# Local attention rebuilt: q and k made by features, their lengths spread from DRAM, tokens weighed instead of values

## The chip, the core and the metric

The kernel runs on one NeuronCore of a Trainium2 chip. The core has a matrix engine (TensorE, "PE" in the profile, its weight loads "PEld"), VectorE ("DVE"), ScalarE ("ACT"), GpSimd ("POOL") and a queue engine (SyncE, "SP") that here issues all DMAs. The engines run side by side; each takes its own instructions strictly in the order of the program and waits on semaphores for the others. Matrix products land in PSUM (eight banks of 2 KB per partition), everything else is in SBUF (128 partitions). The metric is device time in microseconds (us) of one execution.

## The reference

`x` is [8, 512, 128]: 8 batches, 512 tokens, 128 features, all float32. Two blocks follow each other:

- `x = x + LN(attention(LN(x)))`: 16 heads with a Taylor-expanded kernel (1 + s + s²/2, causal). The change doesn't alter its arithmetic.
- `x = x + LN(six layers(LN(x)))`. Each layer is a local attention and a feed-forward, on tokens shifted by one in half of the features:

```
for i in range(6):
    x = attn_layer(shift_tokens(x)) + x
    x = ffn_layer(shift_tokens(x)) + x
attn_layer: q, k, v = split(x @ Wqkv)            # 16 heads of 64
            q = l2norm(q) * qs; k = l2norm(k) * ks
            q = q*cos*scale + rotate_half(q)*sin*scale     # k with 1/scale
            window of 32 tokens: each token sees its window and the one before
            attn = softmax(8 * q k^T, masked);  out = attn @ v;  return out @ Wo
ffn_layer:  (LN(x) @ W1 + b1) -> a * gelu(gate) @ W2 + b2   # inner width 341
```

## The kernel before, in words

**Two stages.** The first (to about 479 us) is the Taylor attention, `slot` and what it calls. The second walks 192 units: 6 layers x 8 batches x 4 blocks of 128 tokens. The state is kept by features in SBUF (`state[b]`, 128 features x 513), so that a shift of tokens is an offset of one column.

**The order.** For TensorE the order is written out by hand: the loop over `t` at the end of the kernel. In turn `t`, `at(t, lag, step)` runs `step` for unit `t - lag`, so several units are in flight, one step each. For the other engines a list scheduler places the instructions; a tile pool gives each tile a buffer by its tag, and an instruction that needs a buffer waits for the last reader of the tile that was there. PSUM has the tags `mm` (two buffers of two banks), `s` (one buffer of two banks: scores, weighed values) and `tr` (two of one bank).

**One unit before**, in turns 0 to 3:

- `proj` (L439): q and k by tokens, four products of 128x128 by 512 columns (L451). VectorE multiplies them by the two tables of the rotation (`turned` L459, `straight` L467), ScalarE squares them (L475; it waits for `straight`), GpSimd adds the two (L482).
- `values` and `spread`: v by tokens (L509), copied by ScalarE (L514) and dealt out by eight DMAs into windows.
- `sum_squares` (VectorE, L485), `unit_length`: a root by logarithm and exponential (L96, L98), a clamp on GpSimd (L495), and q and k times it on GpSimd (L498).
- `by_features`: 16 transposes on TensorE (L70) and four ScalarE copies (L548) bring q and k to features.
- `masked` (L558): ScalarE writes the mask into PSUM; `scores` (L572): 64 small products per unit added onto it; VectorE takes the maxima (L580), 16 exponentials on ScalarE (L584) with the maximum as bias, VectorE the sums (L590).
- `by_keys`: 8 transposes of the weights on TensorE and two copies (L602). `weigh_values`: 64 small products with v (L613), VectorE divides by the sums (L621).
- `out_by_features`: 8 more transposes and two copies (L635). `out_project`: 8 products (L642), VectorE adds to the state (L647).
- After a batch's fourth block: `feed_norm`, `feed_first`, `feed_middle`, `feed_last`, in four turns that follow each other (lags 3 to 6), with Gelu tables loaded and unloaded on ScalarE.

Padding instructions (`addr_align`, lines 668, 671, 780, 782) stand between some matrix products.

Of the kernel before, what the change touches and what calls it, by code (L numbers as in the profile page):

```python
# [8 lines left out]
F32 = mybir.dt.float32  # L9
# [14 lines left out]
FILL = 16  # L24
IN_STEP = 98
# [3 lines left out]
def sandwich_kernel(ctx: ExitStack, tc: tile.TileContext, ins: dict, out: bass.AP):  # L29
# [5 lines left out]
    DEPTH = ins["L0_ffn_Wqkv"].shape[0]  # L35
# [16 lines left out]
    x1 = [dram.tile([P, NB, DM], F32, tag=f"x1_{b}", name=f"x1_{b}") for b in range(B)]  # L52
    roots = [dram.tile([2, 2, 2, N], F32, tag=f"roots_{i}", name=f"roots_{i}") for i in range(2)]
    state = [const.tile([P, N + 1], F32, tag=f"state_{b}", name=f"state_{b}") for b in range(B)]
    for b in range(B):
        nc.vector.memset(state[b][HD:P, 0:1], 0.0)
# [3 lines left out]
    vec = const.tile([P, NV + 1], F32, tag="vec", name="vec")  # L60
    g_c, b_c, b2_c = (vec[:, i * DEPTH : (i + 1) * DEPTH] for i in range(3))
    b1_c = vec[:, 3 * DEPTH : NV].rearrange("p (c l) -> p c l", l=DEPTH)
    gw = vec[:, NV : NV + 1]

# [8 lines left out]
    tables, exps, divisions, copies, pcopies, maxima = [], [], [], [], [], []  # L73
# [7 lines left out]
    def gelu_only():  # L81
        ld = nc.scalar.preload_act_table_set("gelu_and_others")
        issue_behind(ld, pcopies[-1])
        issue_behind(ld, exps[-1])
        tables.append(ld)
# [51 lines left out]
    fq = ctx.enter_context(tc.tile_pool(name="fq", bufs=2))  # L137

    HF = HD // 2
# [13 lines left out]
    tw = wl.tile([P, 3, 2, 512], F32, tag="wqkv", name="tw")  # L153
# [4 lines left out]
    nc.sync.dma_start(tw[:, 2], a_w[:, 2])  # L158
# [3 lines left out]
    woT = tw[:, 2].rearrange("p s (c d) -> p (s c) d", d=DM)  # L162
# [10 lines left out]
    for a in range(2):  # L173
        nc.vector.memset(of[HD * a : HD * (a + 1), a::2], 1.0)
    eps4 = const.tile([P, 1], F32, tag="eps4", name="eps4")
# [54 lines left out]
    def project_qk(G):  # L230
        b, g = divmod(G, NQ)
        k = f2.tile([P, 2, N], F32, tag="pe", name=f"tk_{G}")[:, 0]
        q = fq.tile([P, N], F32, tag="tq", name=f"tq_{G}") if g % 2 == 0 else gr[G - 1]["q"]
        gr[G]["q"], gr[G]["k"] = q, k
        for s, dst in ((0, q), (1, k))[g % 2 :]:
            cols = slice(g * P, (g + 1) * P) if s else slice(g // 2 * P, (g // 2 + 1) * P)
            ps = psum.tile([P, N], F32, tag="tr", name="qk")
            nc.tensor.matmul(ps, wqk[:, s, cols], bt[b]["xlT"], start=True, stop=True)
            nc.scalar.copy(dst, ps)
# [160 lines left out]
    rot = const.tile([P, 4, NB, HD], F32, tag="rot", name="rot")  # L400
    nc.sync.dma_start(rot, ins["rotary"].rearrange("k (n p) d -> p k n d", p=P))
    qks = const.tile([P, 2, DEPTH, HD], F32, tag="qks", name="qks")
    for s, nm in enumerate(("q_scale", "k_scale")):
        nc.sync.dma_start(
            qks[:, s].rearrange("p l d -> p (l d)"),
            ins[f"L0_ffn_{nm}"].rearrange("l d -> (l d)").partition_broadcast(P),
        )

    def load_layer(l):
        wqkv = wl.tile([P, 3, 2, 512], F32, tag="wqkv", name=f"wqkv_{l}")  # L410
        nc.sync.dma_start(
            wqkv, ins["L0_ffn_Wqkv"][l].rearrange("p (t s c) -> p t s c", t=3, s=2)
        )
        wo = wl.tile([P, NP, DM], F32, tag="wo", name=f"wo_{l}")
        nc.sync.dma_start(wo, ins["L0_ffn_Wo"][l].rearrange("(c p) d -> p c d", p=P))
# [7 lines left out]
        tab = wl.tile([P, 4, NB, HD], F32, tag="tab", name=f"tab_{l}")  # L423
        for s in range(2):
            sc = qks[:, s, l, :]
            nc.gpsimd.tensor_tensor(
                tab[:, 2 * s], rot[:, 2 * s], sc.unsqueeze(1).to_broadcast([P, NB, HD]), ALU.mult
            )
            for a, o in ((0, HF), (HF, 0)):
                nc.gpsimd.tensor_tensor(  # L430
                    tab[:, 2 * s + 1, :, a : a + HF],
                    rot[:, 2 * s + 1, :, a : a + HF],
                    sc[:, o : o + HF].unsqueeze(1).to_broadcast([P, NB, HF]),
                    ALU.mult,
                )

        return dict(wqkv=wqkv, wo=wo, w1=w1, w2=w2, tab=tab)

    def proj(u, s):  # L439

        L, b, j = u["L"], u["b"], u["j"]
        wqkv, tab = L["wqkv"], L["tab"]
        lhs = state[b][:, j * P : (j + 1) * P]
        if s == 0:
            u["ss"] = f2.tile([P, 2, H], F32, tag="ss", name="ss")
            u["qk"] = f2.tile([P, 2, H, 2, HF], F32, tag="qk", name="qk")
        ss, qk = u["ss"], u["qk"]

        ps = psum.tile([P, 2, H, HF], F32, tag="mm", name="mm")
        for a in range(2):  # L450
            nc.tensor.matmul(  # L451
                ps[:, a].rearrange("p h d -> p (h d)"), lhs, wqkv[:, s, a, :], start=True, stop=True
            )
        sq = f2.tile([P, H, 2, HF], F32, tag="sq", name="sq")
        t1 = f2.tile([P, 2, H, HF], F32, tag="t1", name="t1")
        t2 = f2.tile([P, 2, H, HF], F32, tag="t2", name="t2")

        def turned():
            nc.vector.tensor_tensor(  # L459
                t2, ps[:, ::-1],  # L460
                tab[:, 2 * s + 1, j, :].rearrange("p (a d) -> p a d", a=2).unsqueeze(2)
                .to_broadcast([P, 2, H, HF]),
                ALU.mult,
            )

        def straight():
            nc.vector.tensor_tensor(  # L467
                t1, ps,
                tab[:, 2 * s, j, :].rearrange("p (a d) -> p a d", a=2).unsqueeze(2)
                .to_broadcast([P, 2, H, HF]),  # L470
                ALU.mult,
            )

        def squared(a):
            nc.scalar.activation(sq[:, :, a, :], ps[:, a], AF.Square)  # L475

        turned()
        straight()
        squared(0)
        squared(1)  # L480
        u["sq", s] = sq
        nc.gpsimd.tensor_tensor(qk[:, s].rearrange("p h a d -> p a h d"), t1, t2, ALU.add)  # L482

    def sum_squares(u, s):
        su = nc.vector.tensor_reduce(  # L485
            u["ss"][:, s], u["sq", s].rearrange("p h a d -> p h (a d)"), AX.X, ALU.add
        )
        if divisions:
            issue_behind(su, divisions[-1])

    def unit_length(u):

        ss, qk = u["ss"], u["qk"]
        inverse_root(ss, ss)
        nc.gpsimd.tensor_scalar(ss, ss, 1e12, None, ALU.min)  # L495
        for i in range(2):
            t = qk[:, i].rearrange("p h a d -> p h (a d)")
            nc.gpsimd.tensor_tensor(  # L498
                t, t, ss[:, i, :].unsqueeze(2).to_broadcast([P, H, HD]), ALU.mult
            )  # L500

    def values(u):
        L, b, j = u["L"], u["b"], u["j"]
        lhs = state[b][:, j * P : (j + 1) * P]

        v0 = f3.tile([P, 2, 512], F32, tag="v0", name="v0")
        ps = psum.tile([P, 2, 512], F32, tag="mm", name="mm")
        for p in range(2):
            nc.tensor.matmul(ps[:, p, :], lhs, L["wqkv"][:, 2, p, :], start=True, stop=True)  # L509
        u["v0"], u["v0ps"] = v0, ps  # L510

    def spread(u):
        j, v0 = u["j"], u["v0"]
        cp = nc.scalar.copy(v0, u.pop("v0ps"))  # L514
        if copies:
            issue_behind(cp, copies[-1])

        v2 = f2.tile([P, 4, 512], F32, tag="v2", name="v2")
        for p in range(2):
            if j == 0:  # L520
                nc.gpsimd.memset(v2[HD * p : HD * p + W, 0, :], 0.0)
            else:
                nc.sync.dma_start(v2[HD * p : HD * p + W, 0, :], u["B"]["v0"][P - W : P, p, :])
            nc.sync.dma_start(v2[HD * p + W : HD * (p + 1), 0, :], v0[0:W, p, :])
            for w in range(1, 4):
                nc.sync.dma_start(
                    v2[HD * p : HD * (p + 1), w, :], v0[W * (w - 1) : W * (w + 1), p, :]
                )
        u["B"]["v0"] = v0
        u["v2"] = v2  # L530

    def by_features(u, c, which=(0, 1)):

        j, qk, B_ = u["j"], u["qk"], u["B"]
        if c == 0:
            u["qT"] = f1.tile([P, NP, P], F32, tag="qT", name="qT")
            if j == 0:
                B_["kT"] = f2.tile([P, NP, W + P], F32, tag="kT", name="kT")
                nc.gpsimd.memset(B_["kT"][:, :, :W], 0.0)
            u["kT"] = B_["kT"]  # L540
        for s in which if isinstance(which, tuple) else (which,):
            ps = psum.tile([P, 4, P], F32, tag="tr", name="tr")
            for i in range(4):
                h0 = 2 * (c + i)
# [384 lines left out]
```

## Time and profile before

| | |
|---|---|
| time, 3 runs | 3640.79 us median (3638.26 to 3641.88) |
| profiled execution | span 3641.2 us; no other time of it is given |
| first stage | 0 to 479 us (first L451 at 479.0) |
| 192 units | 515 us per layer of 32 units, 16.09 us per unit |
| last L451 to the end | 3564.7 to 3641.2: 77 us |
| PE / DVE / ACT / POOL busy | 98 / 77 / 76 / 51 % |
| DMA | 250.73 MB, mean 69 GB/s; the kernel's own queue 240.93 MB in 25.2% of 16 engines' span |
| tr, 32 per unit (L70) | qk 440.9, pe 217.5, on 209.7 us |

A matrix product in float32 appears as two instructions (two passes), a transpose as one. "Busy" of a group is the time with at least one of its instructions running; the mean is that of one instruction, and they overlap, so a group's busy time and the spacing of starts say what it costs, not the mean. After the bar stands the idle time of the engine before the group, with what ended it. In the timeline a line gives start, duration, engine, line and count; in brackets what it had waited for.

### The profile page before, as it was taken

What the parts mean: (1) busy time and instruction counts of PE and PEld (TensorE: products, weight loads), DVE (VectorE), ACT (ScalarE), POOL (GpSimd) and SP (SyncE); (2) the same over time, 40 slices, a digit from 0 to 9 for tenths busy, and PEclk for the clock granted to TensorE, in tenths of its full rate; (3) what the DMA queues carried; (4) which work ended last, traced back from release to release, by engine and by line L of the source; (5) the groups of instructions that cost most, each with busy time, mean ns of one, the idle gap of its engine ahead of it and who ended that gap; (6) DMA issues with size and microseconds to landing.
All of it is one profiled execution on the core that took longest, in us unless ns stands there. A gap on an engine that the chain in (4) does not pass through costs nothing.

```text
span 3641.2 us, 153034 instructions
## 1 busy us (share of the span) xinstructions
PE 3575.2 (98%) x65184; PEld 2404.3 (66%) x65184; DVE 2796.4 (77%) x3915; ACT 2765.6 (76%) x6864; POOL 1843.6 (51%) x1311
## 2 busy tenths in 40 slices
PE   8999989999999999999999999999999999999997
PEld 4555556666766666676766766667676676766765
DVE  4555567887878788787887878878787887878885
ACT  4555557787888888888787888888878787887875
POOL 0000045555655556555565655556555565556652
PEclk9999999999999999999999999999999999999998
DMA  3121132222232222232222322223222222222221
GB/s 109 46 53 47 42 89 68 65 65 69 79 77 72 65 64 71 77 81 68 61 69 68 87 72 69 65 65 86 71 71 69 60 70 64 66 68 73 74 74 47
DMA packets 158598, 250.73 MB, mean 69 GB/s; under 512 B 33774, under 2 KB 54508, under 8 KB 157164
## 3 DMA queue, kind: packets, MB, share of 16 engines
q1 hardware_dynamic: 157932, 240.93, 25.2%
q8 instruction: 530, 8.68, 1.0%
q14 instruction: 136, 1.11, 0.1%
HBM read 41.31 MB, written 4.46 MB: 13 GB/s over the span
## 4 chain that ended last, share of the span: by engine, by line
PE 87%; ACT 9%; DVE 2%; issue 1%; DMA 1%; POOL 0%; SPq 0%; POOLq 0%; DVEq 0%; ACTq 0%
PE tr L70 19%; PE mm L451 14%; PE py L642 10%; PE mm L509 9%; PE po L613 8%; PE sp L572 6%; ACT pe L584 4%; PE mm L667 4%; PE mm L669 4%; PE y L299 3%; PE py L702 3%; PE sc L269 2%; PE po L348 2%; ACT L76 1%; PE vv L247 1%; ACT oT L635 1%
## 5 line engine op out<-in xcount | busy, mean ns | idle before, releaser
L482 POOL TENSOR_TENSOR qk<-t,t 128x1024 f32<-128x1024 f32 x384 | 910.9, 2372 | 619.1 <-DVE t L467 424.7
L498 POOL TENSOR_TENSOR qk<-qk,ss 128x1024 f32<-128x1024 f32 x384 | 722.4, 1902 | 16.0
L451 PE MATMUL mm<-wqkv,state 128*128 128x512 f32 x1536 | 700.3, 596 | 0.6 <-issue 0.6
L584 ACT ACTIVATE pe<-sp,mx 128x64 f32<-128x64 f32 x3072 | 652.0, 381 | 2.4 <-DVE mx L580 2.3
L459 DVE TENSOR_TENSOR t<-mm,tab 128x1024 f32<-128x1024 f32 x384 | 468.3, 1219 | 220.3 <-PE mm L451 214.9
L475 ACT ACTIVATE sq<-mm 128x512 f32<-128x512 f32 x768 | 420.6, 605 | 127.4 <-DVE t L467 120.9
L467 DVE TENSOR_TENSOR t<-mm,tab 128x1024 f32<-128x1024 f32 x384 | 468.1, 1219 | 5.9
L451 PEld LDWEIGHTS mm<-wqkv,state 128*128 128x128 f32 x1536 | 273.1, 190 | 289.8 <-issue 242.4
L485 DVE TENSOR_REDUCE ss<-sq 128x16 f32<-128x1024 f32 x384 | 448.4, 1209 | 0.1
L70 PE MATMUL tr<-ident,qk 128*128 128x128 f32 x3072 | 440.9, 276 | 1.8 <-ACT qT L548 0.8
L70 PEld LDWEIGHTS tr<-ident,qk 128*128 128x128 f32 x3072 | 351.3, 141 | 120.7 <-issue 56.3
L642 PE MATMUL py<-oT,wo 128*128 128x128 f32 x3072 | 379.3, 277 | 0.3 <-ACT oT L635 0.3
L642 PEld LDWEIGHTS py<-oT,wo 128*128 128x128 f32 x3072 | 368.1, 196 | 0.5 <-ACT oT L635 0.5
L509 PE MATMUL mm<-wqkv,state 128*128 128x512 f32 x768 | 362.9, 595 | 2.6 <-DVE t L467 2.6
L635 ACT COPY oT<-tr 128x512 f32<-128x512 f32 x384 | 205.5, 587 | 168.1 <-PE tr L70 165.5
L572 PEld LDWEIGHTS sp<-kT,qT 64*32 64x32 f32 x24576 | 264.2, 105 | 91.3 <-issue 54.3
L613 PE MATMUL po<-v,pT 64*32 64x64 f32 x24576 | 297.0, 225 | 9.6 <-issue 3.9
L548 ACT COPY qT<-tr 128x512 f32<-128x512 f32 x384 | 226.3, 589 | 99.6 <-PE tr L70 99.1
L613 PEld LDWEIGHTS po<-v,pT 64*32 64x32 f32 x24576 | 268.8, 105 | 46.0 <-PE tr L70 24.6
L572 PE MATMUL sp<-kT,qT 64*32 64x64 f32 x24576 | 297.6, 225 | 0.3 <-issue 0.3
L495 POOL TENSOR_SCALAR ss<-ss 128x32 f32<-128x32 f32 x192 | 54.7, 285 | 478.7 <-ACT ss L98 470.8
L548 ACT COPY kT<-tr 128x512 f32<-128x512 f32 x384 | 225.6, 588 | 74.8 <-PE tr L70 74.5
(110 smaller groups left out, 5243.9 us busy)
## 6 DMA issues: line engine op xcount, KB each, us to landing
v<-v SPq DMA_DIRECT2D x1152, 128.0 KB
v<-v SPq DMA_DIRECT2D x672, 64.0 KB
rs<-roots SPq DMA_DIRECT2D x64, 256.0 KB
wqkv<-in_L_ffn_Wqkv_dram SPq DMA_DIRECT2D x6, 1536.0 KB
wo<-in_L_ffn_Wo_dram SPq DMA_DIRECT2D x6, 512.0 KB
xin<-_attn_hidden_states_dram SPq DMA_DIRECT2D x8, 256.0 KB
xr<-_attn_hidden_states_dram SPq DMA_DIRECT2D x8, 256.0 KB
x<-xr SPq DMA_DIRECT2D x8, 256.0 KB
```

The source lines that it names most:

```text
L70: nc.tensor.transpose(ps[:cols, :rows], src, ident[:rows, :rows])
L451: nc.tensor.matmul(ps[:, a].rearrange("p h d -> p (h d)"), lhs, wqkv[:, s, a, :], start=True, stop=True)
L459: nc.vector.tensor_tensor(t2, ps[:, ::-1], tab[:, 2 * s + 1, j, :].rearrange("p (a d) -> p a d", a=2).unsqueeze(2) .to_broadcast([P, 2, H, ...
L467: nc.vector.tensor_tensor(t1, ps, tab[:, 2 * s, j, :].rearrange("p (a d) -> p a d", a=2).unsqueeze(2) .to_broadcast([P, 2, H, HF]), ALU.mult,)
L482: nc.gpsimd.tensor_tensor(qk[:, s].rearrange("p h a d -> p a h d"), t1, t2, ALU.add)
L498: nc.gpsimd.tensor_tensor(t, t, ss[:, i, :].unsqueeze(2).to_broadcast([P, H, HD]), ALU.mult)
L509: nc.tensor.matmul(ps[:, p, :], lhs, L["wqkv"][:, 2, p, :], start=True, stop=True)
L548: copies.append(nc.scalar.copy(dst, ps))
L572: nc.tensor.matmul(sp[W * w : W * (w + 1), p, pair, :], qT[HD * p : HD * (p + 1), pair, W * w : W * (w + 1)], kT[HD * p : HD * (p + 1), pa ...
L584: ex = nc.scalar.activation(pe[:, pair, p, :], sp[:, p, pair, :], AF.Exp, bias=mx[:, p, pair : pair + 1])
L613: nc.tensor.matmul(po[W * w : W * (w + 1), p, pair, :], pT[r, pair, W * w : W * (w + 1)], v2[r, w, HD * pair : HD * (pair + 1)], start=(pa ...
L642: nc.tensor.matmul(py, L["wo"][:, c, :], oT[:, c, :], start=(c == 0), stop=(c == NP - 1))
```

## The change

Everything in a unit between the state and the residual is rebuilt; the first stage changes only in where its tiles lie. A unit now spans turns 0 to 5, feed-forward lags are 5 to 8, and two turns more drain the end.

- q and k are made by features at once: the weights are the stationary operand, the tokens move. 16 products of 128x128 by 128 columns. The 16 transposes and their copies go. Rotated halves lie on other partitions now, so `t2` is moved between groups of 32 partitions by four DMAs for each of q and k.
- Squares are summed over partitions by 16 narrow products (`ms`); the clamp is on VectorE; two small DMAs write the reciprocal lengths to DRAM, and four DMAs of 256 KB read them back, spread over 64 partitions each. GpSimd multiplies by them.
- The exponential: VectorE subtracts the maxima (`pe`), ScalarE takes one exponential of 1024 columns. GpSimd divides. VectorE turns the weights in blocks of 32x32 (`pT`).
- Instead of values, the state's own tokens (`x`, two transposes) are weighed: 8 products of 32x128 by 512 columns (`z`), copied by two ScalarE instructions. Value and output weights are multiplied per head once a layer (`value_products`, 16 products), and `out_project` has 16 products per unit, in two halves around `z`.
- `feed_norm` copies to SBUF first; the padding instructions go; the next layer's weights are loaded half a layer ahead; the rotary tables are read per layer and scaled on GpSimd.

```diff
     def proj(u, s):
...
+        for c in range(NP):
+            nc.tensor.matmul(
+                ps[:, c], L["wqk"][:, s, c * P : (c + 1) * P], state[b][:, tok], start=True, stop=True
+            )
...
+        nc.vector.tensor_tensor(t2, ps, tab[1], ALU.mult)
...
+        for q in range(4):
+            nc.sync.dma_start(tu[W * (q ^ 1) : W * ((q ^ 1) + 1)], t2[W * q : W * (q + 1)])
+        straights.append(nc.vector.tensor_tensor(t1, ps, tab[0], ALU.mult))
+        with tc.high_priority():
+            squared_last.append(nc.scalar.activation(sq, ps, AF.Square))
+        nc.gpsimd.tensor_tensor(u["qk"][:, s], t1, tu, ALU.add)
+    def sum_squares(u):
+        u["ms"] = ms = psum.tile([P, 2, P], F32, tag="tr", name="ms")
...
+                    nc.tensor.matmul(
+                        ms[W * i : W * (i + 1), s], per_head[:, r], sq[:, 2 * i + r],
...
+    def unit_length(u):
...
+            inverse_root(rt, u.pop("ms"))
+            nc.vector.tensor_scalar(rt, rt, 1e12, None, ALU.min)
+        rd = lengths[u["j"] % 2]
+        for a in range(2):
+            nc.sync.dma_start(rd[a].rearrange("s c n -> c s n"), rt[8 * a : P : 16])
+        rs = [f1.tile([P, NP, P], F32, tag=("qT", "rs")[s], name="rs") for s in range(2)]
+        for s in range(2):
+            for a in range(2):
+                nc.sync.dma_start(
+                    rs[s][HD * a : HD * (a + 1)].rearrange("p c n -> p (c n)"),
+                    rd[a, s].rearrange("c n -> (c n)").partition_broadcast(HD),
                 )
...
+        nc.gpsimd.tensor_tensor(u["qk"][:, 0], u["qk"][:, 0], rs[0], ALU.mult)
+        nc.gpsimd.tensor_tensor(u["kT"][:, :, W:], u["qk"][:, 1], rs[1], ALU.mult)
...
+    def by_tokens(u):
...
+        ps = psum.tile([P, 2, P], F32, tag="tr", name="tx")
...
+        nc.scalar.copy(x, ps)
     def scores(u):
...
+            nc.vector.tensor_tensor(
+                pe.rearrange("t c p k -> t p c k"), sp,
+                mx.unsqueeze(3).to_broadcast([P, 2, NP, 2 * W]), ALU.add,
+            )
+        ex = nc.scalar.activation(pf, pf, AF.Exp)
+    def divided(u):
+        sm = nc.vector.tensor_reduce(su, pe, AX.X, ALU.add)
...
+        nc.gpsimd.tensor_tensor(pe, pe, su.unsqueeze(3).to_broadcast([P, NP, 2, 2 * W]), ALU.mult)
+    def by_keys(u):
+        turned = nc.vector.transpose(
+            pT.rearrange("k h a t -> k (h a t)"), u["pe"].rearrange("t c p k -> t (c p k)")
+        )
+    def weigh_tokens(u):
...
+        ps = [
+            psum.tile([P, 2, H, W], F32, tag="s", name="z", bufs=1),
+            psum.tile([P, 2, H, W], F32, tag="mm", name="z"),
+        ]
+                nc.tensor.matmul(
+                    ps[w // 2][:, w % 2], x[r, a, :], pT[r, :, a, :], start=(a == 0), stop=(a == 1),
...
+                nc.scalar.copy(zT[:, :, 2 * i : 2 * i + 2, :].rearrange("f h w t -> f w h t"), ps[i])
+    def out_project(u, half):
...
+        for h in range(half * NP, (half + 1) * NP):
+            nc.tensor.matmul(
+                py, L["wm"][:, h % 2, h // 2, :], zT[:, h].rearrange("f w t -> f (w t)"),
...
     def feed_norm(u):
+        nc.scalar.copy(xn, ps)
+        u["normed"] = layer_norm(f2, xn, xn, NB, by_log=True, later=True)
...
             at(t, 0, proj, 0)
             at(t, 0, proj, 1)
+            at(t, 2, divided)
+            at(t, 5, out_project, 0)
+            at(t, 4, weigh_tokens)
             at(t, 1, masked)
+            at(t, 3, by_keys)
+            at(t, 5, out_project, 1)
+            at(t, 3, by_tokens)
+            at(t, 0, sum_squares)
+            at(t, 0, unit_length)
+            at(t, 5, feed_norm, ends=True)
+            at(t, 6, feed_first, ends=True)
+            at(t, 7, feed_middle, ends=True)
+            at(t, 8, feed_last, ends=True)
             at(t, 1, scores)
```

Removed are `values`, `spread`, `by_features`, `weigh_values`, `out_by_features` and the exponentials with a bias.

## The prediction

> **What bounds the kernel now.** Read in this order: the engines' shares, the chain that ended last, windows by stage, groups by shape, then single turns in the timeline.
>
> ```profile
> PE 3575.2 (98%) x65184; PEld 2404.3 (66%) x65184; DVE 2796.4 (77%) x3915; ACT 2765.6 (76%) x6864; POOL 1843.6 (51%) x1311
> ...
> PE 87%; ACT 9%; DVE 2%; issue 1%; DMA 1%; POOL 0%; SPq 0%; POOLq 0%; DVEq 0%; ACTq 0%
> ```
>
> TensorE is busy nearly always and carries 87% of the chain. Windows (columns: length, then busy PE, PEld, DVE, ACT, POOL with counts, granted clock, DMA share, GB/s):
>
> ```profile
> 494.00:498.00 4.00, 1.22 (x4) 0.93 (x4) 3.87 (x4) 0.38 (x1) 0.33 (x1) 0.63 0.94 198
> 498.00:502.00 4.00, 3.22 (x16) 3.23 (x17) 1.75 (x2) 0.71 (x2) 2.94 (x1) 0.52 0.08 18
> ...
> 1532.00:2047.00 515.00, 513.82 (x10324) 354.75 (x10324) 416.22 (x529) 418.44 (x1081) 303.31 (x214) 1.00 0.27 71
> ```
>
> The third is one layer: 16.09 us per unit, TensorE stands 1.2 us in 515. A turn before is TensorE's own work. The first two are for the clock, below.
>
> ```profile
> L451 PE MATMUL mm<-wqkv,state 128*128 128x512 f32 x1536 | 700.3, 596 | 0.6 <-issue 0.6
> L70 PE MATMUL tr<-ident,qk 128*128 128x128 f32 x3072 | 440.9, 276 | 1.8 <-ACT qT L548 0.8 <-ACT kT L548 0.7 <-ACT pT L602 0.3
> L642 PE MATMUL py<-oT,wo 128*128 128x128 f32 x3072 | 379.3, 277 | 0.3 <-ACT oT L635 0.3
> L509 PE MATMUL mm<-wqkv,state 128*128 128x512 f32 x768 | 362.9, 595 | 2.6 <-DVE t L467 2.6
> L613 PE MATMUL po<-v,pT 64*32 64x64 f32 x24576 | 297.0, 225 | 9.6 <-issue 3.9 <-PE tr L70 0.8 <-PE py L642 0.7
> L269 PE MATMUL sc<-tq,tk 32*128 32x512 f32 x256 | 40.1, 640 | 0.0
> L324 PE MATMUL ms<-ysq,of 128*32 128x512 f32 x128 | 17.0, 605 | 0.0
> ```
>
> Each busy time over 192 units (or the count) prices the products. Last, turns in the timeline:
>
> ```profile
> 59.85 1.14 SPq L334 DMA_DIRECT2D roots<-rt  x4
> 61.44 2.43 SPq L338 DMA_DIRECT2D rs<-roots  x4
> 66.48 1.28 DVE L340 SCALAR_TENSOR_TENSOR yT<-yT,vec,rs 128x1024 f32<-128x1024 f32 x1 [1.93 <-DMA rs<-roots]
> ...
> 490.20 3.76 POOL L498 TENSOR_TENSOR qk<-qk,ss 128x1024 f32<-128x1024 f32 x2
> 492.25 2.79 DVE L340 SCALAR_TENSOR_TENSOR yT<-yT,vec,rs 128x1024 f32<-128x1024 f32 x1 [3.70 <-DMA rs<-roots]
> ...
> 1506.47 1.23 DVE L467 TENSOR_TENSOR t<-mm,tab 128x1024 f32<-128x1024 f32 x1
> 1507.73 1.08 ACT L475 ACTIVATE sq<-mm 128x512 f32<-128x512 f32 x2 [0.67 <-DVE t L467]
> ...
> 3285.09 3.76 POOL L498 TENSOR_TENSOR qk<-qk,ss 128x1024 f32<-128x1024 f32 x2
> 3288.20 1.51 DVE L112 TENSOR_SCALAR fo<-fo,ln_mv,ln_rs 128x128 f32<-128x128 f32 x4
> 3289.68 1.22 DVE L459 TENSOR_TENSOR t<-mm,tab 128x1024 f32<-128x1024 f32 x1
> 3290.82 1.22 DVE L467 TENSOR_TENSOR t<-mm,tab 128x1024 f32<-128x1024 f32 x1
> ```
>
> See: a Square starts only when `straight` has ended; VectorE's wide instructions start 1.14 apart; lengths need 6.6 us from the root's end to the first spread tile in use; and a VectorE instruction that met a running GpSimd one ended 1.08 after it (2.79 against 1.28).
>
> **TensorE's work, part by part (us per unit).** Gone: values 1.89, 30 transposes net (4.52 less 0.29 for `tx`), weighed values 1.55. Added: eight more output products 1.98; `z` 8 products at 40.1/32 = 1.25 per four, 2.5; `ms` 1.06 (as many columns as one L324 group of four, 17.0/16); `proj` 16 products at 1.98 per eight, 3.95 against 3.65. Net -1.83, so 14.26 of 16.09. Were the strips of `z` not to overlap, 16 passes of 0.43 would make 6.9; I take 2.5, the row of the same shape.
>
> **What takes its place.** From one end of `scores` to the next the new order is one chain through three engines, since on ScalarE the two Squares, the copy of `z`, the mask, the second copy and the copy of `x` stand in that order, and `ms` reuses the bank of `tx`, so it waits for the last of them:
>
> - VectorE: maxima 1.23 and subtraction 1.23 (row L621), 0.05 ahead of each, then turned and straight for q, the same for k, 1.14 apart, the last 1.22: ends at 7.1.
> - ScalarE: Square of k 1.02, copy, mask, copy at 1.02 (L514, L558), 0.1 of overlap where nothing is awaited, `x` 0.38 (between 0.24 at 32 and 0.59 at 512 columns): 11.35. TensorE has been done with `z` at 7.8 and, after the second half of the output, waits from about 10.
> - TensorE: `ms` 1.06, `scores` 1.5, 0.1: **14.0**.
>
> Feed-forward stands between `ms` and `scores`, so it adds whole: middle 5.5 (1524.90 to 1530.36 in the chain), last 2.74 and 0.15, first 0.6, norm 0.6 plus VectorE's statistics (0.85 past the end of `scores`) and four `xn` of 0.29 ahead of the next turn: 11.6 per four turns, 2.9 each. Sum 16.9.
>
> Then the port. `xn` and the clamp of the lengths now go from SBUF to SBUF, as L112 on `fo` at 3288.20, which ended 0.1 after GpSimd's product. GpSimd has four products of 2.37, one of 1.90 and a copy of 0.40 per turn, 11.8, busy some 70%: a mean wait of 0.8, between 0 and 2.37. It counts in the norm turn twice and in the first turn partly: 1.9 per four, **0.45**. Behind the clamp in VectorE's queue stand the statistics or the maxima, and for the clamp itself SP's two writes of the lengths.
>
> Sum 17.35 a turn; 192 x (17.35 - 16.09) = +242. Per layer five times 7: the 16 weight products 1.8, two copies on ScalarE's chain 2.0, four table products on GpSimd 2.9 (L426); +35. Two more turns of drain hold little but a wait or two: +5. 3641.2 + 282 = 3923; the profiled span is 0.4 above the median: **3925**.
>
> **Costed at nothing.** VectorE's transpose: 1.21 (the reduction L590 reads as much) to twice that; VectorE waits from 10.3 to 13.4 in each turn. GpSimd's 11.8 and SP's 14 issues of 0.28 to 0.6 (8 us): under the 17; if the turn were 12, GpSimd would bind. The spread lengths: root ends 0.95 after `ms`, clamp 0.3, 6.6, 1.2 for the second pair of DMAs, two products 4.7: 13.8, against 14.0 and the feed-forward's share before the next `scores`; queued behind them on SP are the next unit's `t2` moves, and behind those GpSimd's sums. With the division between the two products it is 15.7, in turns that have 2.6 to 5.5 to spare. DMA bytes double to some 2 MB a unit, at 240.93 MB in 25.2% of the span (263 GB/s full) 8 of 17 us. 3767 padding instructions of 13 ns: 49 us of TensorE's queue at most, gained only where it binds; lost, should they have helped fetching, at most the chain's 1% of issue, 36. I take 0.
>
> **Rivals.**
>
> 1. *TensorE stays the bound* (faster). For it: 98%. Against: the waits above. 192 x (14.26 - 16.09) + 40 = -311: 3330. It decides where the loop with feed-forward takes under 15.9 (16.09 less 40/192), that is 1.0 below my 16.9 with the port at nothing: one ScalarE copy off the chain would do. Between: 3330 to 3634. Chance 0.10.
> 2. *GpSimd's round.* If the clamp always has to wait for both sums, clamp 0.3, 6.8 to the spread tile and GpSimd's 11.8 follow each other: 18.9 a turn, +540 + 40: 4220. For it: the rows of the port; against: VectorE may slip in between two GpSimd instructions. Chance 0.17.
> 3. *The clock.* TensorE stands some 3 us a turn. After waits of 2.56 and 2.46 the granted clock was 0.63 and 0.52 above, and in the drain eight output products took 3.42 (at 3601.47) instead of 1.95. At half speed for 3 us a turn, 1.5 more: 18.9, 4220; at none, nothing. I take nothing, since a turn's waits come in pieces of 1 to 2 us, and after the drain's shorter ones (0.73, 0.29, 0.36) the record shows 1.00; both ends stay in the range. Chance 0.15 that it costs 1 us a turn or more. [...]
> 4. *Nothing changes*: every step of the unit is replaced, so the change can't fail to act; that gains and losses cancel within 0.2% (what a measurement of this kernel can tell from no change) 0.03.
>
> **How the numbers follow.** My forecast has 0.55: 3765 to 4055 (turn 16.5 to 18.0: port wait 0 to 1, 0.5 either way in the chain). Faster 0.10, same 0.03, slower 0.87, being the sum of forecast, 2 and 3. The range reaches to 3630, where the chain breaks even, and to 4290, 70 us, a third of a microsecond a turn, above rivals 2 and 3; about 0.1 is left out below and 0.1 above.
>
> **What would show it.** TensorE busy near 80 to 85% with idle time ahead of `ms`, put down to the ScalarE copy of `x`; the chain shared by VectorE, ScalarE and TensorE; Squares waiting for `straight`; clamp and `xn` with maxima well over their medians; `z` near 2.5 a unit. Wrong if idle before `scores` goes to GpSimd (rival 2), the clock under 0.95 (3), TensorE over 95% (1), or `z` near 7.

## The result

The changed kernel takes 4011.4 us (median of four executions, 4003.8 to 4024.4) against 3641.3 before: a ratio of 1.102, 95% interval 1.100 to 1.104, or +370 us. Forecast were 3925 us, in a range of 3630 to 4290. The profiled execution has a span of 4006.9 us, 1.7 us under its own time of 4008.6, which is 2.8 under the median.

The page of the changed kernel, the shares and then the chain by engine and by line (these answer to the first fence of the prediction):

```profile
PE 3542.8 (88%) x51168; PEld 2568.2 (64%) x51168; DVE 2901.8 (72%) x3928; ACT 1892.1 (47%) x2508; POOL 2283.4 (57%) x1203
...
DVE 26%; PE 22%; ACT 18%; issue 8%; DMA 8%; SPq 3%; POOL 3%; DVEq 0%; POOLq 0%; ACTq 0%
DVE t L460 6%; DVE t L465 6%; DVE rt L489 5%; ACT sq L467 5%; PE ms L478 5%; PE z L588 5%; DMA rs<-lengths 4%; ACT zT L595 3%; ACT sp L526 3%; DVE mx L548 3%; PE py L604 3%; PE mm L453 3%; DMA tu<-t 3%; PE sp L540 3%; ACT x L519 2%
```

TensorE was busy for 98% and carried 87% of the chain; now it is busy for 88% and carries 22%. It lost only 32 us of busy time (3575.2 before), though it has 14,000 instructions less, and it waits for 464 us. What stands in the chain is the round that was forecast: `turned` and `straight` on VectorE, the Squares, the two copies of `z`, the mask and the copy of `x` on ScalarE, `ms` on TensorE. One entry is larger than it was meant to be: `rt` L489, the limit of the lengths (the prediction's clamp), a VectorE instruction on 128x256 elements.

The waits of TensorE (us in all, times, longest) name the same round:

```profile
PE ms L478 <- ACT x L519: 216.3, 187, 1.5
PE z L588 <- ACT sq L467: 93.5, 80, 2.9
PE sp L540 <- POOL kT L506: 62.4, 23, 7.6
```

`ms` waits for the copy of `x` in 187 of 192 turns. And here is one turn in the timeline (start, duration; times in us):

```profile
2007.06 1.21 DVE L465 TENSOR_TENSOR t<-mm,tab 128x1024 f32<-128x1024 f32 x1
...
2008.19 1.21 DVE L460 TENSOR_TENSOR t<-mm,tab 128x1024 f32<-128x1024 f32 x1
...
2009.33 1.21 DVE L465 TENSOR_TENSOR t<-mm,tab 128x1024 f32<-128x1024 f32 x1
...
2010.63 1.02 ACT L467 ACTIVATE sq<-mm 128x1024 f32<-128x1024 f32 x1 [1.24 <-DVE t L465]
...
2011.55 1.01 ACT L595 COPY zT<-z 128x1024 f32<-128x1024 f32 x1
...
2012.59 1.02 ACT L526 CAST sp<-mask 128x1024 f32<-128x1024 bf16 x1
...
2013.54 1.01 ACT L595 COPY zT<-z 128x1024 f32<-128x1024 f32 x1
...
2014.45 0.38 ACT L519 COPY x<-tx 128x256 f32<-128x256 f32 x1
...
2014.88 1.08 PE L478 MATMUL ms<-sq,per_head 128*32 128x128 f32 x32 [1.24 <-ACT x L519]
...
2016.29 4.72 POOL L468 TENSOR_TENSOR qk<-t,tu 128x1024 f32<-128x1024 f32 x2
...
2016.89 1.90 DVE L489 TENSOR_SCALAR rt<-rt 128x256 f32<-128x256 f32 x1 [2.85 <-ACT rt L99]
...
2018.71 0.86 DVE L108 BATCH_NORM_STATS2 ln_st<-xn 128x6 f32<-128x128 f32 x4
```

Down to `ms` each instruction starts where the one above it ends: VectorE's last `straight`, the Square of k, copy, mask, copy, `x`, `ms`. Then the limit: it starts at 2016.89, while GpSimd runs the first of its two sums (from 2016.29), and ends at 2018.79, when that sum is over. The statistics of the layer norm stand behind it in VectorE's queue. The first L453 starts at 478.9, the last at 3918.3, so a turn takes 18.01 us (before, by L451, 16.16).

Turns differ by what feed-forward adds. From one end of `scores` to the next, in the trace, a turn took on average 15.87 us with the norm, 18.13 with `feed_first`, 20.92 with `feed_middle` and 16.81 with `feed_last` (43 or 44 turns each). The parts of the prediction give 14.6, 16.6, 19.5 and 16.9, without its 0.45 for the wait on GpSimd (its "port"). So the chain of 14.0 is met where only `feed_last` stands in the turn; the other three are 1.3 to 1.5 us longer.

### The profile page after: what moved, and what is told of

Same layout as the page of the kernel before. It is cut to its first block, busy times and chain, and to the rows that moved or that the text cites. A ratio compares the mean times of both kernels' runs of the same rounds, so it can differ in the third digit from the quotient of the medians.

```text
span 4006.9 us, 117817 instructions
## 1 busy us (share of the span) xinstructions
PE 3542.8 (88%) x51168; PEld 2568.2 (64%) x51168; DVE 2901.8 (72%) x3928; ACT 1892.1 (47%) x2508; POOL 2283.4 (57%) x1203
## 4 chain that ended last, share of the span: by engine, by line
DVE 26%; PE 22%; ACT 18%; issue 8%; DMA 8%; SPq 3%; POOL 3%; DVEq 0%; POOLq 0%; ACTq 0%
DVE t L460 6%; DVE t L465 6%; DVE rt L489 5%; ACT sq L467 5%; PE ms L478 5%; PE z L588 5%; DMA rs<-lengths 4%; ACT zT L595 3%; ACT sp L526 3%; DVE mx L548 3%; PE py L604 3%; PE mm L453 3%; DMA tu<-t 3%; PE sp L540 3%; ACT x L519 2%
## 5 line engine op out<-in xcount | busy, mean ns | idle before, releaser
L468 POOL TENSOR_TENSOR qk<-t,tu 128x1024 f32<-128x1024 f32 x384 | 901.5, 2366 | 28.4 <-DMA tu<-t 27.8
L604 PEld LDWEIGHTS py<-zT,wm 128*128 128x128 f32 x6144 | 747.4, 199 | 159.4 <-issue 159.3
L604 PE MATMUL py<-zT,wm 128*128 128x128 f32 x6144 | 800.9, 286 | 0.0
L453 PE MATMUL mm<-state,wqk 128*128 128x128 f32 x6144 | 755.2, 282 | 7.9 <-issue 7.7
L453 PEld LDWEIGHTS mm<-state,wqk 128*128 128x128 f32 x6144 | 716.7, 195 | 28.6 <-issue 12.1
L505 POOL TENSOR_TENSOR qk<-qk,rs 128x1024 f32<-128x1024 f32 x192 | 453.6, 2362 | 476.9 <-DMA rs<-lengths 476.3
L588 PE MATMUL z<-pT,x 32*128 32x512 f32 x3072 | 565.8, 643 | 95.1 <-ACT sq L467 93.5
L489 DVE TENSOR_SCALAR rt<-rt 128x256 f32<-128x256 f32 x192 | 346.9, 1807 | 411.1 <-ACT rt L99 411.1
L467 ACT ACTIVATE sq<-mm 128x1024 f32<-128x1024 f32 x384 | 393.3, 1024 | 525.7 <-DVE t L465 399.0
L506 POOL TENSOR_TENSOR kT<-qk,rs 128x1024 f32<-128x1024 f32 x192 | 453.0, 2359 | 19.7 <-DMA rs<-lengths 14.0
L478 PE MATMUL ms<-sq,per_head 128*32 128x128 f32 x6144 | 210.5, 278 | 222.5 <-ACT x L519 216.3
L595 ACT COPY zT<-z 128x1024 f32<-128x1024 f32 x384 | 386.2, 1007 | 8.0 <-PE z L588 8.0
```

The costliest lines, as they stand in the source:

```text
L453: nc.tensor.matmul(ps[:, c], L["wqk"][:, s, c * P : (c + 1) * P], state[b][:, tok], start=True, stop=True)
L467: squared_last.append(nc.scalar.activation(sq, ps, AF.Square))
L468: nc.gpsimd.tensor_tensor(u["qk"][:, s], t1, tu, ALU.add)
L478: nc.tensor.matmul(ms[W * i : W * (i + 1), s], per_head[:, r], sq[:, 2 * i + r], start=(r == 0), stop=(r == 1), skip_group_check=True,)
L489: nc.vector.tensor_scalar(rt, rt, 1e12, None, ALU.min)
L505: nc.gpsimd.tensor_tensor(u["qk"][:, 0], u["qk"][:, 0], rs[0], ALU.mult)
```

## The experiments

All are the changed kernel with one or more edits; where lines were added, line numbers are up to six higher than in the changed kernel. Times are medians, with the ratio to the kernel before and its interval.

| run | edits | us | ratio |
|---|---|---|---|
| e1_clamp_psum | limit from PSUM | 3894.9 | 1.069 (1.068 to 1.071) |
| e2_xn_psum | layer norm from PSUM | 3948.8 | 1.083 (1.080 to 1.087) |
| e3_x_early | early x | 3944.0 | 1.083 (1.081 to 1.085) |
| e4_fill | transposes of the tokens four times | 3842.9 | 1.056 (1.053 to 1.058) |
| f1_order | orders laid down on GpSimd and SP | 3944.1 | 1.083 (1.080 to 1.085) |
| f2_order_fill | orders, transposes four times | 3787.3 | 1.040 (1.038 to 1.042) |
| f3_order_x | orders, early x | 3748.0 | 1.028 (1.024 to 1.032) |
| f4_order_x_clamp | orders, early x, limit | 3672.4 | 1.010 (1.006 to 1.014) |
| g1_bank | orders, fixed banks | 3806.3 | 1.046 (1.044 to 1.049) |
| h1_no_xn | orders, early x, limit, tables on ScalarE | 3648.6 | 1.002 (1.001 to 1.003) |
| g3_all | as h1, and layer norm from PSUM | 3582.9 | 0.984 (0.982 to 0.985) |
| g4_bank_all | as g3, fixed banks for early x | 3763.2 | 1.034 (1.032 to 1.036) |

**e1: the limit from PSUM.**

```diff
-            inverse_root(rt, u.pop("ms"))
-            nc.vector.tensor_scalar(rt, rt, 1e12, None, ALU.min)
+            nc.vector.tensor_scalar(rt, u.pop("ms"), 1e-24, None, ALU.max)
+            inverse_root(rt, rt)
```

> The changed kernel, with the limit of the lengths taken ahead of the logarithm (from PSUM, max 1e-24) in place of behind the exponential (from SBUF to SBUF, min 1e12); VectorE has as many instructions. Port theory: the limit (mean 1807 ns in the changed kernel) comes to 0.3 to 0.45 us; the statistics, the maxima and the two writes of the lengths behind it come 1.4 us sooner; where it stands ahead of the maxima that is 0.7 to 1.4 us off a turn's chain, so 192 x 0.7 to 1.4: 3740 to 3880, best 3810. Rival (the wait was slack, since GpSimd's round or the lengths' way through DRAM ends last anyway): the limit gets short and the time stays within 30 us of 4011.

117 us were won, a little less than the theory's least (131). The line's own instruction, in the changed kernel (minimum, median, maximum in ns):

```profile
L489 DVE TENSOR_SCALAR rt<-rt x192: 283/1896/2521, 489.0 to 3928.3; 128x256 f32<-128x256 f32 x192
```

and in this run:

```profile
L488 DVE TENSOR_SCALAR rt<-ms x192: 385/425/426, 490.0 to 3816.1; 128x256 f32<-128x256 f32 x192
```

The same size from SBUF to SBUF took anything from 0.28 to 2.5 us, from PSUM to SBUF always 0.4, though GpSimd was running at its start in 190 of the 192 turns. And in the changed kernel 188 of the 192 end between 0.1 and 0.2 us after a GpSimd instruction has ended. So the spread is the wait for GpSimd. That the whole 117 us come of it doesn't follow: the scheduler also placed GpSimd's division otherwise (by the starts in the traces, ahead of both products in 26 turns, not in 53; e3 tells why that matters). With the division's place laid down the same edit won 76 us (f4 against f3).

**e2: the layer norm from PSUM**, as in the kernel before.

```diff
-        nc.scalar.copy(xn, ps)
-        u["normed"] = layer_norm(f2, xn, xn, NB, by_log=True, later=True)
+        u["normed"] = layer_norm(f2, xn, ps, NB, by_log=True, later=True)
```

> The changed kernel, with the layer norm of the feed-forward reading PSUM as in the kernel before (no ScalarE copy, xn written from PSUM). Port theory for xn: its mean falls from 432 ns to 0.3 us and the ScalarE copy of 0.57 us goes: (4 x 0.14 + 0.6) us in each of 48 norm turns, 4011 - 55 = 3955, at least 3940 to 3995. Rival: the PSUM buffer of mm is held until xn, 4 us longer than until the copy, and the next turn's q or k product waits for it: no gain, 4000 to 4100.

63 us won, where 55 were expected. But the order moved here too: in the trace the division stands ahead of both products in 9 turns, not in 53, and the orders alone are worth as much (f1). The rival's wait came as well: TensorE's q and k products waited 107 us for `xn`. So this run doesn't price the layer norm's form; g3 against h1 does.

**e3: x early.** `at(t, 3, by_tokens)` moves from behind `out_project` to right behind `proj`.

> The changed kernel, with the two transposes of the tokens moved from behind the output product to the place right behind the q and k products of the same turn; nothing else in TensorE's order moves. ScalarE then copies x ahead of the two Squares, and ms waits for TensorE and the Squares alone. Chain theory (five ScalarE instructions between the last Square and ms set the turn): idle time ahead of ms put to x goes from 216 us to near 0, and a turn gets shorter by up to 2.3 us, what the mask's end still allows, less what GpSimd and the lengths' way take: 1.0 to 2.3 us a turn, 3570 to 3820, best 3700. Rival (GpSimd's round, or the lengths, end just behind): idle time moves from ms to scores, put to GpSimd's kT; less than 100 us gained, 3910 to 4011.

Only 67 us: the rival's number. The waits of TensorE show that both were at work. The idle time ahead of `ms` went (5.9 us are left), and this came in its place:

```profile
PE sp L540 <- POOL kT L506: 317.7, 108, 6.8
```

GpSimd in the timeline says why kT is late:

```profile
2133.68 1.90 POOL L569 TENSOR_TENSOR pe<-pe,su 128x1024 f32<-128x1024 f32 x1 [8.07 <-DVE su L568]
2135.53 2.35 POOL L505 TENSOR_TENSOR qk<-qk,rs 128x1024 f32<-128x1024 f32 x1
2137.84 2.39 POOL L506 TENSOR_TENSOR kT<-qk,rs 128x1024 f32<-128x1024 f32 x1
```

The division stands ahead of the two products by the lengths. It waits 8 us for VectorE's sums, which come late in the turn, and the products wait behind it, though they need nothing of it. Nobody wrote this order: the list scheduler places it by its own estimates, and the edit of TensorE's order shifted them. By the starts in the traces, the division stands ahead of both products in 126 turns here, in 53 of the changed kernel (the expectations below have a count that is a few lower, 119 and 49). In the same way SP's first move of the next unit's turned half stands ahead of reads of the spread lengths in 112 turns here and 53 there; that move waits for the next turn's VectorE.

**e4: fill.** The two transposes of the tokens are made four times over, so TensorE has 1 us more to do per unit.

> The changed kernel, with the two transposes of the tokens made four times over (six more TensorE transposes a unit, of 0.16 us each, 1.0 us a unit) right ahead of the copy of x. Chain theory: TensorE waits there anyway, idle time ahead of ms falls from 216 us by 100 or more, and the time stays within 40 us of 4011; if gaps at TensorE cost clock, the granted clock rises over 0.969 and the time falls. Rival (TensorE's own work sets the end): 192 x 1.0 more, 4200.

Both theories missed: with more work the kernel was 168 us *faster*. The chain theory had left room for a win if the clock rose, and it did rise, from 0.969 to 0.974. The next runs ask why.

**f1 and f2: the orders laid down, without and with the fill.** The division of a unit is made to issue behind the last product by the lengths of the unit after it, the moves behind the last read of the spread lengths:

```diff
+        dv = nc.gpsimd.tensor_tensor(pe, pe, su.unsqueeze(3).to_broadcast([P, NP, 2, 2 * W]), ALU.mult)
+        issue_behind(dv, products[-1])
...
+            mv = nc.sync.dma_start(tu[W * (q ^ 1) : W * ((q ^ 1) + 1)], t2[W * q : W * (q + 1)])
+            if spreads:
+                issue_behind(mv, spreads[-1])
```

> The changed kernel with two orders laid down that its list scheduler had left to its estimates: on GpSimd the division of a turn stands behind the two products by the lengths (in the changed kernel it stands ahead of both in 49 of some 190 turns and between them in 92), on SP the moves of the next unit's turned halves stand behind the four reads of the spread lengths (one of them stands ahead in 52 turns). No instruction is added or left out. Order theory (the run with the four-fold transposes won 168 us because the scheduler, told of more TensorE work, placed the division and the moves better: ahead in 13 and 16 turns): 3760 to 3890, best 3840. Rival (it won by filling TensorE's gaps, so by the clock): 3980 to 4040.

> The two laid-down orders and, with them, the four-fold transposes of the tokens. Order theory: filling alone costs or wins little where ScalarE's copy of x ends last anyway: within 60 us of the run with the orders alone. Clock theory: 100 us or more under it. TensorE's own work as the bound: 100 to 190 us over it.

The orders alone won 67 us, between the two guesses. The fill won another 157 us on top, so the orders weren't its secret. That number is the clock theory's, and the clock did rise, from 0.970 to 0.979; but e4's timeline shows another cause, which g1 then tests by itself:

```profile
2018.22 1.04 PE L72 MATMUL tx<-ident,state 128*128 128x128 f32 x8
2018.42 0.59 DVE L614 TENSOR_TENSOR state<-py,state 64x128 f32<-64x128 f32 x2 [0.40 <-PE py L604]
...
2019.18 1.08 PE L478 MATMUL ms<-sq,per_head 128*32 128x128 f32 x32
2019.42 0.37 ACT L519 COPY x<-tx 128x256 f32<-128x256 f32 x1
```

`ms` starts *before* the copy of `x`. So it no longer lies in the bank of `tx`. The pool of PSUM tiles had, with other estimates, given it the bank of `py`, which VectorE's addition to the state (2018.42) frees. In e4's trace `ms` starts ahead of that copy in 188 turns, in the changed kernel in one, and it waits for VectorE some 187 times more. The fill looks like an edit of the banks in disguise.

**g1: the banks fixed.** `py` and `ms` share one bank of the pair, `tx` has the other; no fill, x as late as ever. (The two feed-forward tiles of the pair go with `tx`, and the first stage's tiles take the two in turn; that stage is no longer, its first L456 starts at 477.6.)

```diff
-        u["ms"] = ms = psum.tile([P, 2, P], F32, tag="tr", name="ms")
+        u["ms"] = ms = psum.tile([P, 2, P], F32, bufs=1, tag="tr0", name="ms")
...
-        ps = psum.tile([P, 2, P], F32, tag="tr", name="tx")
+        ps = psum.tile([P, 2, P], F32, bufs=1, tag="tr1", name="tx")
```

> The two laid-down orders and, with them, fixed PSUM banks: the output py and the sums ms share one bank of the pair, the turned tokens tx have the other (in the changed kernel the pool puts ms into the bank of tx). No transposes added, x copied as late as in the changed kernel. By the wait lists of the programs, the four-fold transposes had also moved ms to the bank of py, so ms there waits for VectorE's addition to the state and no more for ScalarE's copy of x. Bank theory: ms starts about 1.2 us sooner each turn without any filling: 3660 to 3790, best 3730, that is at or up to 126 us (the filling's own busy time) under the filled run's 3787. Filling theory (it won by keeping TensorE busy and its clock up): 3900 to 3960, as with the orders alone.

3806: 138 us under f1 without any filling, 16 over the bank theory's range and 94 under the other's. g1 has a new, shorter wait, which in f2 the filling covers:

```profile
PE ms L483 <- DVE state L620: 103.1, 187, 0.6
```

So freeing `ms` of ScalarE's copy was worth 138 us, most of the 157, and the filling in itself added no more than some 19 (g1 against f2), which covering this wait may explain.

**f3 and f4: the orders with early x, then with the limit too.**

> The two laid-down orders and, with them, the early transposes and copy of x. Chain theory (with the copy of x behind four other ScalarE instructions off the way to ms, up to 2.3 us a turn are won, as long as GpSimd doesn't bring kT late; alone the early copy won only 67 us since the scheduler then put the division ahead of the products in 119 turns, and scores waited 318 us for kT): 190 to 400 us under the run with the orders alone, 3430 to 3650, and the idle time of scores put to kT under 100 us. Rival (the lengths' way itself, root to spread tile to products, ends last): idle of scores put to kT stays above 200 us and the time over 3720.

> The orders, the early x and the limit taken from PSUM ahead of the logarithm. Port theory: another 40 to 130 us under the run without the last, since VectorE gets to the maxima and SP to the lengths earlier by what the limit waited for GpSimd; rival (slack): within 25 us of it.

Early x wins 196 us once kT is not late (its wait is 47.5 us now), the least that the chain theory asked. The time stays over that theory's 3650, where the rival had put it, but the rival's wait for kT didn't come. The limit wins another 76 us, 0.40 us a turn. One thing more differs between the two traces: in f3 GpSimd's memset of the next batch's kT stands ahead of both sums in 37 turns, in f4 in 2. TensorE's waits for kT hardly changed (47.5 and 43.6 us), so most of the 76 is put to the limit, but the two weren't run apart. In f4 TensorE is at 94%, and the chain is its own again:

```profile
PE 3437.2 (94%) x51168; PEld 2584.6 (71%) x51168; DVE 2686.8 (73%) x3928; ACT 1899.0 (52%) x2508; POOL 2273.4 (62%) x1203
...
PE 57%; ACT 9%; DVE 9%; issue 4%; DMA 4%; POOL 2%; SPq 1%; DVEq 0%; POOLq 0%; ACTq 0%
```

**g3, h1 and g4: what is left of waits.** g3 takes the layer norm from PSUM, as e2, and puts the scaling of the rotary tables on ScalarE; h1 leaves the layer norm as the change has it; g4 is g3 with the fixed banks instead of early x.

```diff
-            nc.gpsimd.tensor_scalar(tab[:, k], tab[:, k], qk_c[:, k // 2, l : l + 1], None, ALU.mult)
+            nc.scalar.activation(tab[:, k], tab[:, k], AF.Copy, scale=qk_c[:, k // 2, l : l + 1])
```

> The orders, the early x, the limit from PSUM, the layer norm's xn from PSUM, and the four products that scale the rotary tables on ScalarE in place of GpSimd. What is left of waits over the run with the first three (3672): xn 2.3 us a norm turn, 48 times, of which 0.5 to 1 us is on the way, 20 to 50 us; kT up to 7.8 us late five times, where the table products stand in GpSimd's queue, up to 35 us: 3590 to 3650, best 3620. Rival (TensorE's own 94% is the bound and the waits only move): 3650 to 3680.

> As the run before, with the fixed banks in place of the early x, so the transposes and the copy of x stay late. Bank theory: the copy of x matters to ms alone, so either way of freeing ms gives the same time within 30 us. Rival (the early copy also feeds z or takes load off the end of the turn): 40 us or more slower than the run before.

> The orders, the early x, the limit from PSUM and the table products on ScalarE, but the layer norm of the feed-forward as in the changed kernel (ScalarE copies to SBUF, xn from SBUF to SBUF). It splits the 89 us between the run with the orders, early x and limit (3672) and the run with everything (3583). If the layer norm's form makes most of it (xn took 656 ns against 403, four times in 48 turns, and the copy of 0.57 us stands ahead of the statistics): 3630 to 3665. If the tables make most of it (five waits of scores for kT of up to 7.8 us, 35 us at most), or if the later release of the bank (80 us of waits of the k products for xn) eats what the form wins: 3580 to 3620.

g3 is faster than both kernels: 3582.9 us, 1.6% under the kernel before and 7 us under the least that was expected. h1 splits the last 89 us: 24 for the tables (give or take some 15, since f4's times spread from 3662 to 3692), 66 for the layer norm's form, as its first theory had it. The `xn` of h1 and, below it, of g3:

```profile
L114 DVE TENSOR_SCALAR xn<-xn,ln_mv,ln_rs x192: 329/335/2418, 620.3 to 3622.5; 128x128 f32<-128x128 f32 x192
```

```profile
L114 DVE TENSOR_SCALAR xn<-nx,ln_mv,ln_rs x192: 399/402/411, 620.2 to 3565.3; 128x128 f32<-128x128 f32 x192
```

From SBUF it is shorter at the median and up to 2.4 us long; from PSUM it always takes 0.4. g3 pays for it with a wait of 80 us of the k products for the bank of the norm, which h1 doesn't have, and still wins. g4 is 180 us slower than g3, so the two ways of freeing `ms` are not worth the same, as the rival had it: with the banks fixed, the addition to the state stands between the last output product and `ms` in each turn (104 us of waits in its trace again), with early x nothing does. In g4 `z` is also busy for 38 us more (460.8 against 422.6); the rest of the 180 stays open. The other three edits together won 165 us with early x (f3 to g3) and only 43 with the fixed banks (g1 to g4): what an edit is worth depends on which wait ends last.

## Why the prediction was right, and where its sizes were off

The direction, the mechanism and the range held. The forecast lay 86 us low; the measured turn of 18.01 us stands at the upper end of its 16.5 to 18.0. Point by point:

- **TensorE's work.** `ms` took 1.10 us a unit (210.5 / 192) where 1.06 was taken, `proj` 3.93 (755.2) against 3.95, the output products 4.17 (800.9) against 3.95, `z` 2.95 (565.8) against 2.5. The strips of `z` do overlap: in f4, where it waits less, it takes 2.53, far from the bound of 6.9. In the changed kernel's trace it took 2.63 in the turns without a wait in it and at full clock, 3.09 in those with a wait, 4.28 where the clock had also fallen.
- **The chain** was sized well. From the first maxima of that turn (2003.53) to the end of the last `straight` at 2010.54 were 7.01 us, forecast 7.1 (the steps listed there add up to 7.2); from there to the end of the copy of `x` 4.29, forecast 4.25; then `ms`. That its last link, from the copy of `x` to `ms`, sets the turn is shown by g1 against f1 (138 us), which in the loop changes nothing but the banks; VectorE, ScalarE and GpSimd run in the same order in both traces. f3 against f1 (196 us) agrees, but early x also takes the transposes and the copy out of the end of the turn.
- **The wait for GpSimd** (the prediction's "port") came, and its term was short: 0.45 us a turn for limit and `xn` together, from a mean wait of 0.8 us. The traces show the wait (188 of 192 limits end 0.1 to 0.2 us after a GpSimd instruction) and not what holds VectorE up; "port" is a name here, nothing measured. The limit's mean was 1.81 us, so a wait of 1.5; reading PSUM won 0.40 us a turn (f4 against f3) and the layer norm's form, with its ScalarE copy, 0.34 (g3 against h1). The flaw is in "a mean wait of 0.8": it took GpSimd's place in the turn as random. But its two sums come at the same place in every turn, and in the turn shown its two sums run just when `ms` has ended and the limit comes. Some GpSimd instruction was running at the limit's start in 191 of 192 turns, and the limit's median was 1.9 us. `xn` was caught in only 14 of its 192 instructions.
- **Costed at nothing: the orders of GpSimd and SP.** The text put the division *between* the products at worst (15.7 us) and SP's reads ahead of the next moves. In the trace the division also stands ahead of both, in 53 turns, and a move ahead of reads in 53. Laying both orders down won 67 us, 0.35 a turn (no run splits the two). This is the step that failed outright: the order of each engine could be read before the run, and a late instruction at the head of a queue costs what it waits for, not what it takes (8.07 us against 1.90 for the division in e3's timeline).
- **The table products** were priced at 2.9 us for four, by L426. They took 1.56 each, 6.2 for four, in f4, and behind their own DMA; moving them won 24 us in five layers, where they were taken into a sum of 35; its other terms, the weight products and their copies, no run took apart.
- **Sum.** Forecast turn, with the per-layer 35 us, 16.16 + (242 + 35) / 192 = 17.60; measured 18.01. 0.41 us in 191 turns is 78 us. From the last L453 to the end were 88.6 us, before 76.5, so the drain cost 12 where 5 were taken: with those 7 it is 85. The misses of the wait for GpSimd (0.29) and of the orders (0.35) alone are 0.64, more than the 0.41, so that the sum came nearer than its parts is in some measure luck. They were measured in other surroundings, where a wait that goes uncovers the next, so they don't add up exactly.
- **The rivals.** TensorE as the bound (3330) came nearest in g3, where early x and the rest make it so: yet it takes 3583. Its own work is larger than the 14.26 us taken: in f4 a turn with nothing but one feed-forward product of 2.77 us took 15.06 (2005.50 to 2020.56) without a wait, so 12.3 us for the unit itself; with the forecast's 9.6 us of feed-forward products in four turns that is 14.7. g3 takes 15.83 a turn (first L454 at 481.6, last at 3504.3); the rest, over 14.7, are waits and the clock. GpSimd's round: VectorE does get in between two GpSimd instructions (at the median the limit ends 0.15 us after the one that ran when it came), and `scores` waited for kT only 62 us, so its full form didn't come. The clock: 0.969 granted, 0.993 before. By busy time that is 3542.8 x 0.031 = 110 us against 25, so an estimate of 85 us, under half a microsecond a turn; no run here holds the clock alone fixed, so how much of it is on the path stays open. The reason for taking nothing, that waits of 1 to 2 us leave the clock up, was weak: the eight output products of 3.42 us in the drain of the kernel before stood behind waits of 1.57 and 0.69, and the rows of 0.63 and 0.52 are one fall, behind the wait of 2.56.

Of the signs that were named, these showed: idle time ahead of `ms` put to `x`, the chain shared by three engines, Squares waiting for `straight` (279 times, 399 us), `xn` with a maximum of 2.38 us over a median of 0.34, the clock above 0.95. These differed: the limit's median was itself long, `z` was at 2.95, and TensorE was busier (88%) than the 80 to 85% named.

## What to carry to other kernels

Where a scheduler orders the other engines and a pool gives out the banks, read both from the program before pricing a change: which instruction stands at the head of each queue in each turn and what it waits for, and whose bank each tile takes. An experiment that adds or moves work changes both too, so compare orders and waits of the two programs before believing that it tested what it was meant to. Here a VectorE `tensor_scalar` from SBUF to SBUF beside a busy GpSimd took up to 2.5 us (the limit; 0.28 at the least), from PSUM always 0.4: such an instruction should be priced at the GpSimd instruction that will be running then, or be written to read PSUM.

## What the runs showed of the hardware

**Which VectorE instructions waited for GpSimd.** In the changed kernel's loop only `tensor_scalar` from SBUF to SBUF did (283 to 2521 ns for the limit, 329 to 2377 for `xn`). The 32x32 transpose, the reduction, the reciprocal (213 to 255) and the statistics (268 to 296), all from SBUF to SBUF, did not:

```profile
L573 DVE STREAM_TRANSPOSE pT<-pe x192: 1184/1186/1247, 546.4 to 3958.8; 128x1024 f32<-128x1024 f32 x192
...
L564 DVE TENSOR_REDUCE su<-pe x192: 1202/1208/1220, 527.9 to 3950.0; 128x16 f32<-128x1024 f32 x192
```

A GpSimd instruction was running at the start of 64 of these transposes, 86 of the reductions, 47 of the reciprocals and 176 of the 192 statistics. For the limit it was 191 of 192, for `xn` 14, those that were caught. Why these two waited and the others didn't, the traces don't show.

**The clock fell after waits of some 2 us, but not after each.** In the changed kernel TensorE waited 2.13 us for a Square, up to 2026.70. Windows of 4 us around it (length, busy PE, PEld, DVE, ACT, POOL, granted clock, DMA share, GB/s):

```profile
2018.00:2022.00 4.00, 4.00 (x36) 4.00 (x37) 3.97 (x12) 0.50 (x2) 3.00 (x2) 1.00 0.05 14
2026.00:2030.00 4.00, 3.30 (x14) 1.34 (x15) 3.55 (x5) 2.73 (x4) 2.59 (x2) 0.71 1.02 228
2030.00:2034.00 4.00, 3.72 (x18) 3.32 (x17) 1.45 (x3) 2.04 (x3) 3.94 (x4) 0.50 0.18 39
```

If 0.71 is read as 2.3 us at half, it stood at half for over 6 us (in the trace's clock record from 2027.65 to 2034.48); eight output products took 3.78 us there (at 2029.51) instead of the 2.05 of the turn before. So here the fall came after one wait of 2.1 us, while the wait of 1.24 us ahead of `ms` (up to 2014.88) left the clock at 1.00 (the first window).

The length of one wait doesn't decide alone: of the 20 waits of 2.0 to 2.5 us between 530 and 3920 us, 14 had a fall within 3.5 us of their end, and of the 167 of 1.2 to 1.4 us, 3. In the trace's clock record all falls start on one grid of 3.41 us. In the 3.41 us ahead of a fall after 530 us TensorE was busy for at most 62%; in each of some 900 such stretches at full clock that no fall followed, for at least 49%. So what counts here seems to be how long TensorE stands within one stretch of that grid, with the border somewhere between these two shares; that is an estimate from this one trace, and no run was made to test it.
